# A four-layer graph attention network: other row tiles of layer 2 treated whole, and four early gathers for layer 3

## The chip, the core and the metric

The kernel runs on one core of one Trainium2 chip. The metric is the device time of the whole program in microseconds (us). The engines go by short names: PE is TensorE (PEld its weight loads), DVE is VectorE, ACT is ScalarE, POOL is GpSimd, and SP is the engine whose queue issues plain DMAs. POOL issues the indirect DMAs, called gathers here.

## The reference

A graph of 4096 nodes with 256 features goes through four attention layers, all over one adjacency matrix, in which about one entry in 256 is set, and the diagonal. Each layer adds the input to the attention's output and normalizes. Layers 0 and 1 have four heads of 64 features, layer 2 has two heads of 128. Layer 3 has one head in two signs. Cut to what matters:

```python
def attention(x, adj, ...):                 # layers 0, 1, 2, per head
    e = leaky_relu(s1[:, None] + s2[None, :], 0.2)     # s1, s2: x times learned vectors
    att = softmax(where(adj > 0, e, -huge), axis=1)
    return att @ (x @ W)

def layer3(x, adj, W, a, fc_W):
    e = leaky_relu(Wh1 + Wh2.T, 0.2)
    pos = softmax(where(adj > 0, e, -huge), axis=1)
    neg = -softmax(where(adj > 0, -e, -huge), axis=1)
    return elu(concatenate([pos @ x, neg @ x], axis=1) @ fc_W)

x = layernorm(x + layer_n(x, adj))          # n = 0, 1, 2, 3
```

## The kernel before

**Row tiles, lists, gathers.** The 4096 nodes are 32 row tiles of 128 nodes. As the adjacency is sparse, a row tile needs only the nodes that at least one of its rows is joined to. Beside layer 0 the kernel makes, for every row tile, a list of up to 13x128 such nodes (`lists`), and a packed mask, `maskC`. In a layer a row tile has 14 positions of 128 nodes: 13 are gathered from the table `vals` by the list (L634, POOL), and position 6 (`FRONT`) is the tile's own 128 rows (L631, SP). Positions 0 to 6 are the first half, 7 to 13 the second. The lists are ordered so that positions 0 to 5 name only nodes of row tiles 0 to 16 (`MIX` is 17, `NODES` bounds the source of the gather); the others may name any node. For a half, ACT and DVE make the weights `w` (in layer 3: L664, L665, L667 on ACT, L666, L668 on DVE), and PE multiplies them with the gathered rows (L699 in layers 2 and 3). In layer 3 a first half holds the matmuls of head 1 and then those of head 0, 14 records in the profile for each.

**Whole blocks.** In layers 2 and 3 some row tiles are not gathered but computed against all 4096 nodes, four row tiles (a block) at a time, with a full mask `maskW`. `WHOLE` says how many blocks at the end of the range are treated so: three in layer 2 (row tiles 20 to 31) and one in layer 3 (28 to 31). `whole_rows` yields units, one for each of 32 node tiles (L927 to L938), and `half_with_whole` spreads them over the layer's half steps. While `lists` runs, `places` writes the mask of each such block to DRAM (L392).

**Steps and projections.** A layer walks its gather tiles in half steps, numbered 2m and 2m+1 for the m-th gather tile. A finished row tile is normalized, alone or in groups (`GROUPS`: pairs of an end and a size, looked up by row tile), and joins `ready`. A `Projection` makes its row of the next layer's `vals` table: two transposes (L536, PE), a copy (L541, ACT), the matmuls (L550, PE), the row (L568 to L576, ACT and DVE), its write (L578, SP), then the transposed edge terms (L582, L588, L589). `half_with_whole` starts at most one projection in each half step, in order of `ready`.

**From layer to layer.** `close` ends a layer: it projects what is ready of row tiles below 17, loads the next layer's first half of tile 0, finishes the last tile, computes that half, projects the rest, then loads and computes the first half of tile 1 and loads those of tiles 2 and 3. Second halves are loaded in the steps that follow. Gathered rows land in slots: `g0` has 16, `g1` has 14. In layer 2 a slot holds two positions, in layer 3 one; first halves draw from `g0`, second halves from `g1`, in rotation.

The order written here gives the priorities. Where each engine's and each queue's instructions really stand was fixed when the program was built, by a scheduler that estimates when an instruction can go; on the chip every engine and queue then works strictly in that order.

Of the kernel before, what the change touches and what calls it, by code (L numbers as in the profile page):

```python
# [53 lines left out]
NT = N // P  # L54
KT = F // P
BT = 4
# [16 lines left out]
CAP = NG * P  # L73
HALF = NP // 2

GROUPS = (((24, 4),), ((28, 2),), ((16, 2), (20, 1), (31, 2)), ((28, 1), (31, 4)))
LEAD = 10
MIX = 17
FRONT = 6
# [15 lines left out]

WHOLE = (0, 0, 3, 1)

LEAST = 2.0611536224385579e-09  # L100

# [76 lines left out]
class Turns:  # L178


    def __init__(self, pools):
        self.pools = list(pools)
# [6 lines left out]
class Program:  # L189
# [98 lines left out]
    def lists(self, ctx):  # L288
# [75 lines left out]
        class Block:  # L364
# [23 lines left out]

            def places(self):
                blk = self.blk  # L390
                if blk >= NB - max(WHOLE):
                    nc.sync.dma_start(out=shared["maskW"][blk], in_=self.mk)  # L392
                hit = wk.tile([P, BT, NT], BF16, name="hit")
                nc.vector.tensor_scalar(hit, self.red, 0.0, None, op0=ALU.is_gt)
                flat = hit.rearrange("p t j -> p (t j)")
                nc.vector.memset(flat[:, blk * BT:blk * BT + (BT - 1) * (NT + 1) + 1:NT + 1], 0.0)
                pt = prog.bank(prog.pthree)
                nc.tensor.matmul(pt[:, :P], flat, ones, start=True, stop=True)
                totals = wk.tile([P, P], BF16, name="totals")
                nc.scalar.copy(totals, pt[:, :P])  # L400
                pq = prog.bank(prog.pthree)
                nc.tensor.matmul(pq[:, :P], tri, flat, start=True, stop=False, skip_group_check=True)
                nc.tensor.matmul(pq[:, :P], totals, bt.rearrange("p t j -> p (t j)"), start=False, stop=False,
                                 skip_group_check=True)
                nc.tensor.matmul(pq[:, P:P + BT], totals, tot, start=False, stop=True, skip_group_check=True)
                ms = slice(blk * BT, (blk + 1) * BT)
                self.place = wk.tile([P, BT, NT], F32, name="place")
                here = self.place
                nc.vector.tensor_tensor(here, pq[:, :P].rearrange("p (t j) -> p t j", t=BT), lo[:, ms, :],
                                        op=ALU.subtract)  # L410
                nc.vector.tensor_tensor(here, here, hit, op=ALU.mult)
                nc.vector.tensor_copy(total[:, ms], pq[:, P:P + BT])

                for col in (wid[:, ms, :], None):
                    off = wk.tile([P, BT, NT], F32, name="off")
                    if col is None:
                        nc.vector.tensor_scalar(off, here, 0.0, None, op0=ALU.is_lt)
                    else:
                        nc.vector.tensor_tensor(off, here, col, op=ALU.is_gt)
                    nc.vector.tensor_tensor(bad, bad, off, op=ALU.max)  # L420
# [177 lines left out]
class RowTile:  # L598

    def __init__(self, layer, m):
        self.layer, self.m = layer, m
        self.slots = {}
        self.accs = None

    def place(self, pos):


        L, n = self.layer, self.layer.n  # L610
        per = 1 if n == 3 else 2
        s = pos // per
        if s not in self.slots:
            pool = L.prog.g1 if n > 0 and s * per >= HALF else L.prog.g0
            self.slots[s] = pool.tile([P, 2 * ROW[0]], F32, name="G")
        c = (pos % per) * ROW[n]
        return self.slots[s][:, c:c + ROW[n]]
# [20 lines left out]
    def half(self, half):  # L638
# [1 line left out]
        prog, sh, S = L.prog, L.shared, self.S  # L640
        H, Wd, V, T, A = HEADS[n], WIDTH[n], VALS[n], TERMS[n], LOGS[n]
        if self.accs is None:
            pool = prog.ptwo[1 if n == 3 and self.m % 2 else 0]
            self.accs = [prog.bank(pool) for _ in range(2 if n == 3 else 1)]
        accs = self.accs
        G = [self.place(half * HALF + k) for k in range(HALF)]
# [75 lines left out]
class Layer:  # L722
# [2 lines left out]

    def __init__(self, prog, n):
        self.prog, self.n, self.nc, self.shared = prog, n, prog.nc, prog.shared
        self.count = NT - WHOLE[n] * BT
        self.tiles = {}
        self.loaded = set()  # L730
        self.units = self.whole_rows()
        self.total = WHOLE[n] * NT * (1 if n < 3 else 2)
        self.used = 0
        self.nxt = self.middle = self.stored = self.between = None
        self.group = []
        self.ready = []
        self.step = 0
        self.last = ()


    def tile(self, m):
        if m not in self.tiles:
            self.tiles[m] = RowTile(self, m)
        return self.tiles[m]

    def load(self, m, half):
# [63 lines left out]
    def half_with_whole(self, m, part):  # L810

        proj = None
        self.step = 2 * m + part
        if self.ready and self.ready[0][0] < self.step:
            _, y, row = self.ready.pop(0)
            self.set_banks()
            proj = Projection(self.prog, self.n + 1, self.nxt, y, row)
            proj.transpose()
        with ExitStack() as order:
            for ins in self.last:  # L820
# [27 lines left out]
    def close(self, following):  # L848
# [11 lines left out]
            self.set_banks()  # L860
            Projection(self.prog, self.n + 1, self.nxt, *entry[1:]).all()
        if following is not None:
            following.load(0, 0)
        if WHOLE[self.n]:
            for _ in self.units:
                pass
# [26 lines left out]
    def whole_rows(self):  # L893
        n, nc, prog, sh = self.n, self.nc, self.prog, self.shared
        H, Wd, T = HEADS[n], WIDTH[n], TERMS[n]
        groups = [range(H)] if n < 3 else [(0,), (1,)]
        for blk in range(NB - WHOLE[n], NB):
            tiles = range(blk * BT, (blk + 1) * BT)
            S = prog.bk.tile([P, T, BT, P], F32, name="Sw")
            for it, m in enumerate(tiles):  # L900
# [589 lines left out]
```

## Time and profile before

| what | value |
|---|---|
| median of three runs | 2287.78 us (2284.84 to 2289.15) |
| profiled execution | 2288.18 us |
| its span, first to last instruction | 2286.4 us |
| mean granted clock of PE | 0.961 |
| PE busy | 2026.1 us, 89% |
| PEld busy | 1835.8 us, 80% |
| DVE busy | 1798.3 us, 79% |
| ACT busy | 1741.5 us, 76% |
| POOL busy | 1493.2 us, 65% |
| gathers (L634) | 1456, mean 1017 ns |

The matmuls (L699) of layer 2's gathered half steps run from 1358.0 to 1751 us, and layer 3 fills the rest. A line of a timeline reads: start in us, duration in us (of all, where several instructions are merged), engine, line of the kernel, operation, output <- input, number of instructions, and in brackets the idle time of the engine just before with what ended it. SPq is SP's queue; its time is that of issuing a DMA, not of moving the data.

### The profile page before, as it was taken

The numbers are of one execution on the slowest core, as the hardware profiler recorded it, in microseconds if no ns is written. First come the engines' busy times: TensorE is split into PE (matmuls) and PEld (weight loads), VectorE is DVE, ScalarE is ACT, GpSimd is POOL, SyncE is SP. The second block draws the span as 40 slices with busy tenths as digits, with TensorE's granted clock in tenths as the row PEclk, the third lists the DMA queues.
The fourth block names the chain that finished last, engine by engine and source line by source line (L and its number), as shares of the span: only waits on it lengthen the run. The fifth ranks groups of instructions, "written<-read, shape, count | busy, mean of one in ns | idle before, by whom it ended". The sixth has DMA issues, their size and how long they took to land.

```text
span 2286.4 us, 49074 instructions
## 1 busy us (share of the span) xinstructions
PE 2026.1 (89%) x15689; PEld 1835.8 (80%) x15689; DVE 1798.3 (79%) x5317; ACT 1741.5 (76%) x4977; POOL 1493.2 (65%) x1596
## 2 busy tenths in 40 slices
PE   4888888988999968998889898989998799999996
PEld 2667877877889958998888887989997688888885
DVE  2898998989999968998888895887885365566566
ACT  4778887977789958988788886988883666676664
POOL 2117664646567777777777777777761677777773
PEclk7999999999999989999999999999999899999998
DMA  8889777866456765666666666778764788888884
GB/s 279 257 262 349 219 231 250 282 201 212 143 155 188 208 181 158 190 182 165 177 170 172 176 168 176 221 213 233 217 201 139 243 268 274 270 259 282 261 255 139
DMA packets 250320, 493.00 MB, mean 216 GB/s; under 512 B 44385, under 2 KB 156610, under 8 KB 249666
## 3 DMA queue, kind: packets, MB, share of 16 engines
q0 software_dynamic: 81536, 245.30, 38.0%
q1 hardware_dynamic: 168514, 244.46, 33.5%
q8 instruction: 126, 2.06, 0.4%
q14 instruction: 144, 1.18, 0.2%
HBM read 437.05 MB, written 52.54 MB: 214 GB/s over the span
## 4 chain that ended last, share of the span: by engine, by line
PE 51%; DVE 15%; DMA 14%; ACT 11%; issue 5%; POOL 3%; SPq 0%; DVEq 0%; ACTq 0%; POOLq 0%
PE bank L699 16%; PE bank L696 14%; PE bank L938 10%; DMA G<-vals,idx 8%; ACT w L687 6%; PE bank L550 5%; PE bank L442 4%; POOL G L634 3%; DVE w L688 3%; DMA raw<-in_adjB_dram 2%; DVE w L684 2%; DVE oh L436 2%; DVE w L678 1%; DMA G<-vals 1%; ACT mk L380 1%
## 5 line engine op out<-in xcount | busy, mean ns | idle before, releaser
L634 POOL DMA_INDIRECT G<-vals,idx x1456 | 1480.2, 1017 | 754.2 <-issue 205.0
L687 ACT ACTIVATE w<-S,G 128x128 f32<-128x128 f32 x3248 | 988.2, 389 | 122.9 <-DMA G<-vals,idx 106.8
L696 PE MATMUL bank<-w,G 128*65 128x128 f32 x7168 | 842.9, 277 | 102.0 <-DVE w L684 79.0
L696 PEld LDWEIGHTS bank<-w,G 128*65 128x65 f32 x7168 | 800.6, 140 | 120.8 <-DVE w L684 91.3
L699 PE MATMUL bank<-G,w 128*128 128x257 f32 (+1 forms) x2688 | 491.3, 340 | 33.6 <-DVE w L666 11.8
L699 PEld LDWEIGHTS bank<-G,w 128*128 128x128 f32 x2688 | 431.8, 193 | 83.5 <-DVE w L666 14.7
L688 DVE SCALAR_TENSOR_TENSOR w<-w,bank 128x896 f32<-128x896 f32 x384 | 411.7, 1081 | 21.0 <-ACT w L687 20.5
L938 PE MATMUL bank<-vw,pw 128*128 128x129 f32 (+1 forms) x2048 | 301.2, 304 | 6.6 <-issue 3.2
L938 PEld LDWEIGHTS bank<-vw,pw 128*128 128x128 f32 x2048 | 276.9, 193 | 23.7 <-issue 3.7
L664 ACT ACTIVATE w<-S,G 128x128 f32<-128x128 f32 x392 | 140.0, 391 | 128.7 <-DMA G<-vals 64.3
L436 DVE TENSOR_SCALAR oh<-iota,place 128x256 bf16<-128x256 f16 (+2 forms) x992 | 225.7, 304 | 14.7 <-PE bank L442 14.1
L442 PE MATMUL bank<-mk,oh 128*128 128x132 fp8e4 x2336 | 188.5, 224 | 18.1 <-DVE oh L436 9.2
L550 PE MATMUL bank<-wext,xT 128*128 128x268 f32 (+3 forms) x640 | 181.5, 415 | 16.4 <-ACT xT L541 14.4
L678 DVE TENSOR_TENSOR w<-S,G 128x256 f32<-128x256 f32 x384 | 154.4, 418 | 51.8 <-DMA G<-vals,idx 48.9
L442 PEld LDWEIGHTS <-oh 128*128 128x128 bf16 x2336 | 144.2, 98 | 58.8 <-DVE oh L436 27.3
L380 ACT ACTIVATE mk<-raw 128x1024 uint8<-128x1024 int32 x128 | 130.7, 1053 | 25.8 <-DMA raw<-in_adjB_dram 25.7
L550 PEld LDWEIGHTS bank<-wext,xT 128*128 128x128 f32 x640 | 118.4, 203 | 35.6 <-ACT xT L541 16.9
L927 ACT ACTIVATE pw<-Sw,d 128x512 f32<-128x512 f32 x192 | 131.6, 714 | 17.0 <-PE bank L938 12.7
L935 DVE TENSOR_TENSOR pw<-pw,mw 128x512 f32<-128x512 f32 x64 | 44.0, 692 | 124.3 <-ACT pw L934 65.6
L928 DVE SCALAR_TENSOR_TENSOR pw<-pw,mw 128x512 f32<-128x512 f32 x192 | 126.9, 692 | 18.2 <-ACT pw L927 17.4
L684 DVE SCALAR_TENSOR_TENSOR w<-w,bank 128x896 f32<-128x896 f32 x128 | 138.7, 1083 | 0.9
L688 DVE SCALAR_TENSOR_TENSOR w<-w,mk 128x896 f32<-128x896 f32 x80 | 86.7, 1087 | 43.1 <-ACT w L687 42.0
(131 smaller groups left out, 1605.0 us busy)
## 6 DMA issues: line engine op xcount, KB each, us to landing
raw<-in_adjB_dram SPq DMA_DIRECT2D x128, 512.0 KB
mk<-maskC SPq DMA_DIRECT2D x112, 231.0 KB
G<-vals,idx POOLq DMA_INDIRECT x1456
S<-edge SPq DMA_DIRECT2D x64, 256.0 KB
vw<-vals SPq DMA_DIRECT2D x96, 129.0 KB
xp<-y SPq DMA_DIRECT2D x96, 128.0 KB
y<-xp SPq DMA_DIRECT2D x96, 128.0 KB
mw<-maskW SPq DMA_DIRECT2D x20, 528.0 KB
```

Of the source, the lines that this page charges most:

```text
L380: nc.scalar.activation(mk[:, q:q + 2, :, :P], src, AF.Copy, scale=EDGE)
L436: nc.vector.tensor_scalar(oh[:, :n * P], iota[:, :n * P], self.place[:, it, j:j + 1], None, op0=ALU.is_equal)
L442: nc.tensor.matmul(accs[b][:, s * MC:(s + 1) * MC], oh[:, (k - a) * P:(k - a + 1) * P], mk[:, j, it, :].bitcast(FP8), start=touches[b][0] ...
L550: nc.tensor.matmul(pp[:, :c1 - c0], self.xT[:, k, :], wext[:, k, c0:c1], start=(k == 0), stop=(k == KT - 1 and brow is None))
L634: nc.gpsimd.indirect_dma_start(out=self.place(pos), out_offset=None, in_=sh["v"][n][:NODES[t], :], in_offset=bass.IndirectOffsetOnAxis(ap= ...
L678: nc.vector.tensor_tensor(w[h][:, k:k + 2, :], S[:, h:h + 1, :].to_broadcast([P, 2, P]), dd[:, :, V + T + h:V + T + h + 1].to_broadcast([P ...
L684: nc.vector.scalar_tensor_tensor(w[h], w[h], LEAST, mh, op0=ALU.max, op1=ALU.mult)
L687: nc.scalar.activation(w[h][:, k, :], S[:, h, :], AF.Exp, bias=d(k, h))
L688: nc.vector.scalar_tensor_tensor(w[h], w[h], LEAST, mh, op0=ALU.max, op1=ALU.mult)
L696: nc.tensor.matmul(accs[0][:Wd, h * P:(h + 1) * P], v, w[h][:, k, :], **how)
L699: nc.tensor.matmul(a, w[h][:, k, :], v, **how)
L938: nc.tensor.matmul(accs[it][:, c:c + Wd], p[:, it, :], v[:, c:c + Wd], start=(j == 0 and h == heads[0]), stop=(j == NT - 1), skip_group_ch ...
```

## The change

Three things change.

`WHOLE` now names blocks: 3, 6 and 7 in layer 2, that is row tiles 12 to 15 and 24 to 31. The gather tiles of layer 2 are row tiles 0 to 11 and then 16 to 23, still 20 of them. `ORDER` translates a step into a row tile. The masks written by `places` are those of blocks 3, 6 and 7. The groups of the norm are chosen anew.

`half_with_whole` takes, of the tiles that are ready, those below 17 first.

`close` of layer 2 loads four first halves at once, those of layer 3's tiles 0 to 3. For this, layer 3's slots are dealt anew: tiles 0 and 1 have both halves in `g0`, tiles 2 and 3 have the first half in `g1` and the second in `g0`, and from tile 4 on even tiles are all in `g1`, odd ones all in `g0`.

```diff
-GROUPS = (((24, 4),), ((28, 2),), ((16, 2), (20, 1), (31, 2)), ((28, 1), (31, 4)))
+GROUPS = (((24, 4),), ((28, 2),), ((16, 2), (17, 1), (22, 2), (24, 1), (31, 2)), ((28, 1), (31, 4)))
...
-WHOLE = (0, 0, 3, 1)
+WHOLE = ((), (), (3, 6, 7), (7,))
+ORDER = tuple([m for m in range(NT) if m // BT not in w] for w in WHOLE)
...
-                if blk >= NB - max(WHOLE):
+                if any(blk in w for w in WHOLE):
                     nc.sync.dma_start(out=shared["maskW"][blk], in_=self.mk)
...
         if s not in self.slots:
-            pool = L.prog.g1 if n > 0 and s * per >= HALF else L.prog.g0
+            if n == 3:
+                other = self.step % 2 == 0 if self.step > 3 else self.step > 1 and s < HALF
+            else:
+                other = n > 0 and s * per >= HALF
+            pool = L.prog.g1 if other else L.prog.g0
             self.slots[s] = pool.tile([P, 2 * ROW[0]], F32, name="G")
...
-        self.count = NT - WHOLE[n] * BT
+        self.order = ORDER[n]
+        self.count = len(self.order)
...
-            self.tiles[m] = RowTile(self, m)
+            self.tiles[m] = RowTile(self, m, self.order[m])
...
-        if self.ready and self.ready[0][0] < self.step:
-            _, y, row = self.ready.pop(0)
+        able = sorted((e for e in self.ready if e[0] < self.step), key=lambda e: e[2] >= MIX)
+        if able:
+            self.ready.remove(able[0])
             self.set_banks()
-            proj = Projection(self.prog, self.n + 1, self.nxt, y, row)
+            proj = Projection(self.prog, self.n + 1, self.nxt, *able[0][1:])
...
         if following is not None:
-            following.load(0, 0)
+            for m in range(4 if following.n == 3 else 1):
+                following.load(m, 0)
...
-        for blk in range(NB - WHOLE[n], NB):
+        for blk in WHOLE[n]:
```

More of the change, by code (lines that the diff above doesn't have):

```diff
@@ L598, with __init__ @@
 class RowTile:
-    def __init__(self, layer, m):
-        self.layer, self.m = layer, m
+    def __init__(self, layer, step, m):
+        self.layer, self.step, self.m = layer, step, m
         self.slots = {}
@@ L642, in half @@
         if self.accs is None:
-            pool = prog.ptwo[1 if n == 3 and self.m % 2 else 0]
+            pool = prog.ptwo[1 if n == 3 and self.step % 2 else 0]
             self.accs = [prog.bank(pool) for _ in range(2 if n == 3 else 1)]
@@ L731, in __init__ @@
         self.units = self.whole_rows()
-        self.total = WHOLE[n] * NT * (1 if n < 3 else 2)
+        self.total = len(WHOLE[n]) * NT * (1 if n < 3 else 2)
         self.used = 0
```

## The prediction

> **What bounds the kernel now.** The page came first. Its slice view (40 slices of 57.16 us) shows where an engine falls out of its pattern:
>
> ```profile
> PE   4888888988999968998889898989998799999996
> POOL 2117664646567777777777777777761677777773
> ```
>
> POOL, which issues all gathers, has one hole between its first gathers and its end: slice 31, 1715 to 1772 us. Layer 2 ends there and layer 3 begins. The windows view puts both sides of it in numbers (busy time of PE, PEld, DVE, ACT, POOL, then granted clock, DMA share, GB/s):
>
> ```profile
> 1700.00:1725.00 25.00, 25.00 (x217) 24.69 (x216) 17.50 (x49) 16.64 (x47) 3.75 (x3) 1.00 0.47 139
> 1725.00:1750.00 25.00, 24.92 (x192) 23.69 (x191) 21.76 (x129) 7.80 (x27) 0.00 (x0) 1.00 0.36 113
> 1750.00:1775.00 25.00, 15.96 (x61) 10.45 (x59) 8.88 (x38) 7.39 (x21) 9.91 (x11) 0.80 0.62 181
> 1775.00:1800.00 25.00, 21.57 (x88) 17.82 (x88) 10.77 (x21) 17.03 (x32) 14.55 (x14) 0.86 0.70 216
> 1800.00:1825.00 25.00, 16.86 (x69) 13.81 (x67) 6.97 (x10) 15.99 (x31) 19.21 (x20) 0.86 0.86 263
> 1825.00:1850.00 25.00, 24.95 (x115) 21.90 (x116) 18.86 (x61) 20.01 (x49) 19.40 (x19) 1.00 0.79 244
> ```
>
> Up to 1750 us PE is full. Then it is busy for only 15.96, 21.57 and 16.86 of 25 us, and DVE and ACT are no fuller: something is late. The timelines of POOL and of SP's queue say what:
>
> ```profile
> 1702.80 1.85 POOL L634 DMA_INDIRECT G<-vals,idx  x1 [0.30 <-issue]
> 1762.04 0.94 POOL L634 DMA_INDIRECT G<-vals,idx  x1 [57.39 <-DMA y<-xp]
> ...
> 1787.79 0.95 POOL L634 DMA_INDIRECT G<-vals,idx  x1 [0.30 <-issue]
> 1795.54 1.14 POOL L634 DMA_INDIRECT G<-vals,idx  x1 [6.79 <-issue]
> ```
>
> ```profile
> 1758.22 0.32 SPq L578 DMA_DIRECT2D vals<-row  x1
> ...
> 1791.99 0.37 SPq L578 DMA_DIRECT2D vals<-row  x1
> ```
>
> After layer 2's last gather POOL stands still for 57.4 us. Layer 3's first gather starts 3.82 us after the row write at 1758.22, which is that of row tile 16, the last of the tiles that a first half may read. POOL issues 20 gathers, stands again for 6.79 us, and goes on 3.55 us after the row write at 1791.99: that of row tile 19, the last of all, which every second half must wait for. (Which tile a row belongs to follows from counting projections through the half steps: tile 16 is the first projected in `close`, 31, 17, 18 and 19 come behind.) From 1795.54 on the list of waits holds for POOL
>
> ```profile
> POOL G L634 <- PE bank L699: 36.9, 121, 0.3
> POOL G L634 <- issue: 31.5, 82, 6.8
> ```
>
> and twelve lines like them (us in total, times, longest): but for the 6.8 us just named, no pause is longer than 0.3 us. Of layer 3's 28x13 = 364 gathers, 344 run from 1795.54 to 2257.27 us, (2257.27-1795.54)/344 = 1.342 us each, and 29 us of tail follow. PE is nearly as full, yet POOL never stands: the end of the kernel is the start of POOL's unbroken run, plus gathers left times 1.342, plus the tail. The Trainium skill (Perfetto Trace Analysis, "Identifying the Most-Contended Engine") ranks engines by occupancy, TensorE by its weight loads; in the last window above that is 21.90 of 25 us against POOL's 19.40, so the rule would name TensorE, which these waits contradict. By the rule the 2.3 us charged to POOL below would not count, and the gain would be that much larger.
>
> **Part 1: other whole blocks.** No instruction goes: 20 gather tiles and 96 units stay. Counting half steps by the code's rules, row tile 16 becomes gather step 12 instead of 16 and is projected in half step 29 instead of in `close`. Each half step projects at most one tile. Before, 27 of 32 projections fit into the steps and five remain (16, 31, 17, 18, 19); after, 28 fit and four remain (20, 21, 22, 23). The one more costs PE eight L550 matmuls (1.74 us), transposes and edge (0.36), 2.1 us, in steps where PE is full: step 39's last half ends at 1750.9+2.1 = 1753.0. The groups of the norm stay 18 in number; they cost nothing new.
>
> **Part 2: four first halves at once.** All rows that they read are written some ten half steps before `close`, so POOL waits only for slots, which layer 2's last four gather tiles give back between about 1726 and 1753 us. 24 gathers at 1.25 us (0.95 busy and 0.30 between) are 30 us, and fit into the hole before about 1765. The DMA share of 0.36 to 0.47 there leaves them room.
>
> What then starts POOL's unbroken run is again the last row write. The four projections left are a chain through two banks; their transposes follow each other in 4.21 us in the trace of before (1754.07, 1758.28, 1762.49), and a row's write is issued 4.13 us after its transposes (1758.28 to 1762.41). Before, tiles 17, 18 and 19 fell out of this rhythm (writes at 1770.26, 1778.42, 1791.99), since ACT stood in order at `w` L664 for gathers (24.1 us in 20 waits from 1745 to 1850) and PE ran at a clock of 0.75. These gathers are now there early. Three places for the last write:
>
> - the first-half matmuls fit into the chain's gaps: 1754.07+2.1+3x4.21+4.13 = 1772.9
> - tile 0's half, first in program order and now ready, stands ahead on PE with 6.07 us: 1779.0
> - tile 1's stands ahead as well: 1785.1
>
> I take the middle one, since program order puts only tile 0's half ahead of the four. With 3.55 us to the first gather, second halves start at 1776.5, **1782.6** or 1788.7. Before, 24 gathers were done, and the 25th began, at 1800.85. So POOL gains 24.4, **18.3** or 12.2 us.
>
> **Part 3: the slots.** From step 4 on a tile has 14 slots of one pool, and position p waits for the tile two before, position p (g1) or p-2 (g0), as now or easier. Only the start differs: tile 4's second half takes tile 3's first-half slots, where it took tile 2's second-half slots. Before, this was POOL's 59th gather at 1845.99. Tile 3's first half began on PE at 1844.82, and its second 14 of 28 matmul records, which read each slot last, free the first slot at 1844.82+3.03+0.43 = 1848.3. POOL stands 2.3 us, once; behind it stand all later gathers, and nobody else waits, as tile 4's second half comes on PE some 10 us after its data. On SP's queue the S, mask and own-row loads of tiles 1 to 3 move ahead with their gathers. They wait for buffers that ACT and DVE last read at 1729 and 1736 and for slots free by 1753, so the row writes behind them, of which the one that matters comes after 1765, are not held: I count nothing, and some 8 us (two projections) if SP stood until 1753 with rows behind it.
>
> **Part 4: one mask write moves.** Block 3's 2112 KB go out instead of block 5's. In the trace a `maskW` write is followed by a wait of ACT:
>
> ```profile
> 354.66 0.33 SPq L392 DMA_DIRECT2D maskW<-mk  x1
> ...
> 362.42 0.32 SPq L450 DMA_DIRECT2D maskC<-cm  x1
> ```
>
> ```profile
> 368.93 0.30 ACT L425 COPY cm<-mk 128x132 uint8<-128x132 uint8 x1 [5.71 <-DMA maskC<-cm]
> ```
>
> Such a wait, 5.7, 5.9 and 6.1 us, comes behind each of the three writes; one goes, worth 0 to 5.7 us. The new place is where block 3's totals are cast, 207 us:
>
> ```profile
> 205.00:210.00 5.00, 5.00 (x50) 4.96 (x49) 4.74 (x18) 4.38 (x7) 3.78 (x5) 1.00 1.06 384
> 210.00:215.00 5.00, 2.84 (x27) 2.58 (x26) 3.35 (x14) 0.78 (x2) 3.78 (x5) 1.00 1.04 388
> 215.00:220.00 5.00, 0.25 (x3) 0.01 (x1) 1.11 (x2) 4.24 (x13) 3.78 (x5) 0.83 1.02 386
> ```
>
> The DMA engines are full at 386 GB/s and PE nearly idle, waiting for adjacency. There 2.163 MB cost 2.163/0.386 = 5.6 us if nothing hides them, 0 if layer 0 makes it up later, and 5.6+6.0 if the same wait of ACT comes behind. I take 5.6 against 5.7: nothing, from -5.7 to +11.6. The skill's page DMA: Bandwidth & Descriptors ("Where 436 GB/s comes from") puts HBM's share of a core at about 358 GB/s and the fabric's ceiling at 435. The measured 386 passes the first; by it the write would be an estimated 6.0 us, and by the second an idle reserve of 49 GB/s would take part of it.
>
> **The sum**, against the profiled execution's own 2288.18 us (span 2286.4 and 1.78 around it; the median of the three runs, 2287.78, is 0.4 lower): -18.3 + 2.3 + 0 = -16.0, 2272.2 there and **2272 us** against the median.
>
> **The rivals.** *The last row is no earlier.* PE, ACT and DVE still give tile 23's row at 1792, because units and both first halves stand ahead of the projections. Then POOL starts at 1795.5 with 24 instead of 20 gathers done: -5.3+2.3 = -3, 2285 us, no change to be measured. For it: before, units of layer 3 (L930, L932 on ACT) already slipped between tiles 18 and 19. Against: much of that delay was ACT's wait for gathers.
>
> *Shared slots stop POOL.* This ends slower. First and second halves now draw on one pool; if the pause of 2.3 us comes not once but at every second tile, 12 times, it is 27.6-18.3 = +9.3, 2297 us. It decides from about ten pauses on ((18.3+4.6)/2.3). For it: POOL and PE run almost level, and the 59th gather has no margin. Against: position for position only the first round is tighter.
>
> *PE becomes the bound.* Before tile 0's second half (matmuls from 1815.52) seven units filled PE's holes. If fewer fit, seven times 1.73 us come later, and PE's slack in the run, 6.3 us where it waits for a gather at 1957, takes half: -16+6 = 2278.
>
> **How the numbers follow.** Forecast 0.62, PE as bound 0.15, last row no earlier 0.11, shared slots 0.12. The three runs span 4.3 us, so 0.2% (4.6 us) is about what can be told from no change. The forecast's own ends are -24.4+2.3-5.7 = -27.8 (2260) and -12.2+2.3+11.6 = +1.7 (2289); the far part of the upper end counts as no change. Faster 0.76, same 0.12, slower 0.12. The range goes from 2259 to 2286: it takes in the forecast's lower end, PE as bound and the unmeasurable rival, and leaves out the slower one and the forecast's worst mask write.
>
> **What would show it.** POOL's hole at slice 31 must hold 24 gathers ahead of the last row write. That write must lie near 1779, the next gather 3.5 us behind it, POOL then unbroken but for some 2 us near its 59th gather, its last gather near 2241. ACT's wait behind the first `maskW` write must be gone and the new one stand at about 207 us. A last row later than 1788, or pauses of POOL at every second tile, would prove me wrong.

## The result, and the profile after

The changed kernel takes 2286.56 us (median; 2281.53 to 2292.93) beside 2287.1 us for the kernel before on the same chip: ratio 0.9996, interval 0.9983 to 1.001. That is no change that can be measured; 2272 us was forecast. Its profiled execution took 2287.36 us with a span of 2285.6 us and a mean clock of 0.956. Eight of the runs that follow were on two other chips, on which the kernel before takes 2766 and 2763 us; their times are told only against the kernel before on the same chip.

The slices of the page (PE, then POOL) show that POOL's hole has become two half holes, slices 30 and 31, and PE is no fuller:

```profile
PE   4888898988999959999888996989998889999995
POOL 2117655556567777777777777777773477777773
```

The windows (busy PE, PEld, DVE, ACT, POOL; clock, DMA share, GB/s) show the early gathers: POOL has 15.71 and 12.48 us of work in the first two rows, where it had 3.75 and 0.00 before.

```profile
1700.00:1725.00 25.00, 25.00 (x211) 24.51 (x210) 15.65 (x31) 17.75 (x52) 15.71 (x13) 1.00 0.73 211
1725.00:1750.00 25.00, 21.31 (x152) 20.26 (x151) 20.41 (x111) 13.01 (x39) 12.48 (x12) 0.91 0.83 251
1750.00:1775.00 25.00, 21.23 (x120) 18.36 (x119) 12.72 (x56) 6.99 (x18) 3.89 (x4) 0.96 0.49 148
1775.00:1800.00 25.00, 24.19 (x108) 20.17 (x109) 12.69 (x30) 18.33 (x37) 1.89 (x2) 0.93 0.40 119
```

But PE now loses time already between 1725 and 1750 us (21.31 of 25, full before), and POOL has next to nothing to do from 1775 to 1797. The timelines of POOL and of SP's queue give the reason in three lines each:

```profile
1762.71 1.66 POOL L641 DMA_INDIRECT G<-vals,idx  x1 [6.44 <-ACT w L674]
1764.67 0.94 POOL L641 DMA_INDIRECT G<-vals,idx  x1 [0.30 <-issue]
1797.56 0.94 POOL L641 DMA_INDIRECT G<-vals,idx  x1 [31.95 <-DMA vw<-vals]
```

```profile
1765.86 0.32 SPq L580 DMA_DIRECT2D vals<-row  x1
1776.62 0.32 SPq L580 DMA_DIRECT2D vals<-row  x1
...
1794.28 0.32 SPq L580 DMA_DIRECT2D vals<-row  x1
```

All 24 first-half gathers are out by 1764.67, as forecast ("before about 1765"). Then POOL waits 31.95 us for layer 2's last row, whose write is issued at 1794.28: forecast 1779.0, and 1791.99 before. (The profile puts the wait down to `vw<-vals`, a load issued at 1795.05 that landed last; with both holds, below, it names `vals<-row` itself.) From 1797.56 on POOL runs without a pause over 0.6 us to its last gather at 2254.04; 340 gathers take (2254.98-1797.56)/340 = 1.345 us each, and 30.6 us of tail follow. So POOL's step 25 of layer 3 moved from 1800.85 to 1797.56, 3.3 us, and nothing more reached the end.

A line of ACT's list of waits between 1700 and 1815 us, ACT's timeline and PE's in the same place show what holds the row back:

```profile
ACT w L671 <- DMA G<-vals,idx: 20.4, 11, 4.9
```

```profile
1743.27 0.40 ACT L671 ACTIVATE w<-S,G 128x128 f32<-128x128 f32 x1 [3.13 <-DMA G<-vals,idx]
1745.15 0.40 ACT L671 ACTIVATE w<-S,G 128x128 f32<-128x128 f32 x1 [1.48 <-DMA G<-vals,idx]
...
1746.11 0.15 ACT L570 ACTIVATE row<-bank 128x2 f32<-128x2 f32 x1
...
1759.13 0.40 ACT L671 ACTIVATE w<-S,G 128x128 f32<-128x128 f32 x1 [4.31 <-DMA G<-vals,idx]
```

```profile
1746.99 0.37 PE L584 MATMUL bank<-ident,row 128*1 128x128 f32 x1 [3.69 <-DVE row L578]
...
1770.61 0.38 PE L538 MATMUL bank<-ident,y 128*128 128x128 f32 x2
...
1777.61 0.63 PE L538 MATMUL bank<-ident,y 128*128 128x128 f32 x2
1778.03 2.22 PE L949 MATMUL bank<-vw,pw 128*128 128x257 f32 x6
```

L671 is layer 3's first step for a gathered position, here of tile 1. Of the 20.4 us, 9.2 us in 4 waits lie ahead of the last row write; the rest end from 1801.13 on, behind POOL's restart. These instructions stand in ACT's order ahead of `row` L570, a step of a projection of layer 2. They wait for a gather, the projection waits behind them, PE waits 3.69 us for the projection (`row` L578), and PE holds the end of layer 2 in its own order behind that. Further on, between the transposes L538 of the last four projections, stand matmuls L949: whole units of layer 3. From this came theory R: the last row sets the start of POOL's unbroken run and so the end, and it is late by two parts, ACT's waits ahead of layer 2's last half and units between the last four projections.

### The profile page after: what moved, and what is told of

Its sections match the earlier page's. It is cut to its first block, busy times and chain, and to the rows that moved or that the text cites. A ratio compares the mean times of both kernels' runs of the same rounds, so it can differ in the third digit from the quotient of the medians.

```text
span 2285.6 us, 49078 instructions
## 1 busy us (share of the span) xinstructions
PE 2028.3 (89%) x15689; PEld 1840.9 (81%) x15689; DVE 1798.9 (79%) x5317; ACT 1744.7 (76%) x4977; POOL 1501.1 (66%) x1596
## 5 line engine op out<-in xcount | busy, mean ns | idle before, releaser
L703 PE MATMUL bank<-w,G 128*65 128x128 f32 x7168 | 843.5, 277 | 97.1 <-DVE w L691 79.3
L706 PE MATMUL bank<-G,w 128*128 128x257 f32 (+1 forms) x2688 | 497.7, 343 | 39.9 <-DVE w L695 15.9
L706 PEld LDWEIGHTS bank<-G,w 128*128 128x128 f32 x2688 | 438.3, 196 | 89.3 <-DVE w L695 16.5
L949 PE MATMUL bank<-vw,pw 128*128 128x129 f32 (+1 forms) x2048 | 301.6, 303 | 7.8 <-ACT zw L1013 2.7
L949 PEld LDWEIGHTS bank<-vw,pw 128*128 128x128 f32 x2048 | 275.7, 193 | 25.0 <-ACT zw L1013 3.1
L671 ACT ACTIVATE w<-S,G 128x128 f32<-128x128 f32 x392 | 140.6, 392 | 139.2 <-DMA G<-vals,idx 86.7
L552 PE MATMUL bank<-wext,xT 128*128 128x268 f32 (+3 forms) x640 | 178.2, 409 | 11.5 <-ACT xT L543 9.1
L552 PEld LDWEIGHTS bank<-wext,xT 128*128 128x128 f32 x640 | 117.1, 201 | 28.6 <-ACT xT L543 10.4
```

Of the source, the lines that this page charges most:

```text
L552: nc.tensor.matmul(pp[:, :c1 - c0], self.xT[:, k, :], wext[:, k, c0:c1], start=(k == 0), stop=(k == KT - 1 and brow is None))
L671: nc.scalar.activation(w[0][:, k, :], S[:, 0, :], AF.Relu, bias=d(k, 0))
L703: nc.tensor.matmul(accs[0][:Wd, h * P:(h + 1) * P], v, w[h][:, k, :], **how)
L706: nc.tensor.matmul(a, w[h][:, k, :], v, **how)
L949: nc.tensor.matmul(accs[it][:, c:c + Wd], p[:, it, :], v[:, c:c + Wd], start=(j == 0 and h == heads[0]), stop=(j == NT - 1), skip_group_ch ...
```

## Experiments

**Holding back tile 1, the units, and both.** Each kernel is the changed one with an order put on ACT: tile 1's first half, or the first twelve units of layer 3, or both, may start on ACT only behind the last projection. All computation is kept. The three edits, where `latest` is the last ACT instruction of the latest projection:

```diff
-        nc.scalar.activation(erow[:T, :], self.pe[:T, :P], AF.Identity, ...)
+        one = nc.scalar.activation(erow[:T, :], self.pe[:T, :P], AF.Identity, ...)
+        self.prog.latest = one.ins
...                                   # tile 1 held, in close
-            following.tile(1).half(0)
+            with ExitStack() as order:
+                if following.n == 3:
+                    order.enter_context(self.prog.tc.issue_after(self.prog.latest))
+                following.tile(1).half(0)
...                                   # units held, in whole_rows
+                            with ExitStack() as order:
+                                if heads[0] == 0 and j < 12:
+                                    order.enter_context(prog.tc.issue_after(prog.latest))
-                            nc.scalar.activation(p, S[:, 0], AF.Relu, bias=d)
+                                nc.scalar.activation(p, S[:, 0], AF.Relu, bias=d)
```

They ran first on one of the two other chips. Expected of tile 1 held:

> Starts from the changed kernel; ACT's work for the first half of layer 3's tile 1 may stand on ACT only behind the last projection of layer 2. Theory R (the last row write starts POOL's unbroken run, and that run sets the end): in the changed kernel ACT waits 9.2 us for tile 1's gathers between layer 2's last projections, and layer 2's last half ends at 1762.8 us; here it ends near 1754, the last row write moves from 1794.3 to about 1784.5, POOL goes on near 1788, the time falls by about 10 us to 2277. Theory E (PE is the bound, the row write does not matter): the time stays within 4 us of 2286.6.

of the units held:

> Starts from the changed kernel; the first 12 units of layer 3's whole block may stand on ACT only behind the last projection of layer 2. Theory R: the last four projections come 4.2 us apart instead of 5.5 to 7.0, the last row write moves from 1794.3 to about 1787.5, the time falls by about 6 us to 2280. Theory E: the eight units that filled PE before 1800 us (8 x 1.73 = 14 us) come later and the time rises, to 2290 to 2300.

and of both:

> Both holds of k1 and k2 together. Theory R: last row write near 1778, POOL goes on near 1781, 24 gathers done before that, time 16 us lower, 2270; up to 6 us more if PE then becomes the bound because the units come later (2276). Theory E: 2286 to 2300.

There they took 0.9973 (0.9952 to 0.9993), 0.9973 (0.9951 to 0.9996) and 0.9962 (0.9943 to 0.9981) of the kernel before. The expected absolute times were for the first chip and say nothing here; the changed kernel was not beside them, so these runs show a gain and not yet where it comes from. Tile 1 and the units were run once more on the second of these chips,

> Only ACT's work for tile 1's first half is held behind the last projection. Both holds together gave 2277.45, 9.0 us below the changed kernel. Theory R with its two parts (ACT's waits for tile 1's gathers ahead of layer 2's last half; units of layer 3 between the last four projections): layer 2's last half ends some 9 us earlier than in the changed kernel, the last four projections stay at 5.5 to 7 us each, the last row is written at 1783 to 1786, and the time is 5 to 7 us below the changed kernel. Rival A (only ACT's waits matter): the whole 9 us, the same as both holds. Rival U (only the units matter): within 2 us of the changed kernel.

> Only the first twelve units of layer 3 are held behind the last projection. Theory R: layer 2's last half ends as late as in the changed kernel, the last four projections close up to some 4.5 to 5 us each, the last row is written at 1786 to 1789, and the time is 3 to 5 us below the changed kernel. Rival A (only ACT's waits matter): within 2 us of it. Rival U (only the units matter): the whole 9 us.

with 0.9958 (0.9938 to 0.9979) and 0.9973 (0.9947 to 0.9998): both intervals lie below 1, and the two can't be told from each other there. On chips where the kernel before takes 2287 to 2291 us, and with the changed kernel beside them, the three were run again.

Both held:

> The changed kernel with two holds: ACT's work for tile 1's first half, and the first twelve units of layer 3, stand behind the last projection. Theory R: the last four projections run at about 4.2 us each, the last row is written 10 to 16 us earlier than in the changed kernel, POOL's unbroken run starts as much earlier, and the time falls by 8 to 15 us against the changed kernel of this chip. Rival E (PE is the bound, since the work held back is done later on PE): within 3 us of the changed kernel, though the last row is earlier. Rival A (the delay is ACT's waits ahead of layer 2's last half, and holds behind it don't matter): -2 to -6 us.

Measured: 2277.45 us beside 2286.45 of the changed kernel and 2289.53 of the kernel before, 0.9948 (0.9929 to 0.9967) of the latter: 9.0 us below the changed kernel. The last row write on SP's queue and POOL's restart:

```profile
1779.95 0.32 SPq L580 DMA_DIRECT2D vals<-row  x1
```

```profile
1783.32 0.94 POOL L642 DMA_INDIRECT G<-vals,idx  x1 [28.74 <-DMA vals<-row]
```

The last row is written at 1779.95 and POOL restarts at 1783.32; the prediction had 1779.0 and 1782.6 for the changed kernel. The last half of layer 2 ends at 1752.5 (forecast 1753.0), and the transposes of the last four projections follow each other in 4.18, 4.21 and 5.09 us (forecast 4.21). In the one profile of the changed kernel on this chip the last half ends at 1760.3, the last row is written at 1792.19 and POOL restarts at 1795.59. ACT has no wait for a gather ahead of the last row any more. Rival E (no gain, as PE is the bound) falls: the time follows the restart, though not in full.

Tile 1 held alone:

> Only ACT's work for tile 1's first half is held behind the last projection. Theory R with two parts (ACT's waits ahead of layer 2's last half, units between the last projections): 5 to 7 us below the changed kernel of the same chip, layer 2's last half some 9 us earlier, the last four projections as far apart as in the changed kernel. Rival A (only ACT's waits matter): 9 us below it. Rival U (only the units matter): within 2 us of it.

Measured: 2281.05 us beside 2286.84 of the changed kernel, 5.8 less. ACT's waits for gathers ahead of the last row are gone (the 9.0 us of the list below all end from 1792.75 on, behind POOL's restart), and layer 2's last half ends at 1751.3, where it ends at 1763.2 and 1763.8 in the changed kernel's profiles on this chip; but the last four transposes stand at 1759.04, 1769.88, 1775.04 and 1780.67, even farther apart, as a step of a unit stands 6.4 us for a load there:

```profile
ACT w L672 <- DMA G<-vals,idx: 9.0, 12, 1.8
ACT pw L945 <- DMA Sw<-edge: 6.4, 1, 6.4
```

```profile
1785.51 0.32 SPq L580 DMA_DIRECT2D vals<-row  x1
```

The changed kernel has 1794.57 and 1795.06 on this chip. Units held alone:

> Only the first twelve units of layer 3 are held behind the last projection. Tile 1 held alone was 5.8 us below the changed kernel, both holds 9.0. Theory R (two parts that add): layer 2's last half as late as in the changed kernel, the last four projections some 4.5 to 5 us apart, and 2 to 4.5 us below the changed kernel of the same chip. Rival O (the parts overlap: units that are held give place to ACT's waits, or the other way round): within 1.5 us of the changed kernel, or 5 us and more below it.

Measured: 2283.01 beside 2287.03 of the changed kernel, 4.0 less. Here the last half ends late (1761.0) and ACT's waits stay (11.6 us in 5 waits for gathers ahead of the last row), but the last transposes are 4.12, 4.99 and 6.26 us apart, 15.4 us in all instead of 19.0:

```profile
1790.45 0.32 SPq L580 DMA_DIRECT2D vals<-row  x1
```

The steps do not stay at 4.2 us. Without the units PE is busy for only 3.54 and 4.05 us in the two windows of 5 us from 1775 to 1785, the granted clock in them is 0.53 and 0.50, and the eight matmuls L552 of a projection take 3.81 us, where they take 2.01 at 1769.96:

```profile
1779.40 3.81 PE L552 MATMUL bank<-wext,xT 128*128 128x256 f32 x8 [0.52 <-ACT xT L543]
```

5.8 and 4.0 make 9.8, both together gave 9.0. By the spread of the runs, an estimate, each of these differences is uncertain by some 3 to 5 us, so the times alone exclude "only the units" (within 2 us with tile 1 held) but not "only ACT's waits". The row writes are clearer: they come 9.3 us earlier with tile 1 held, 4.4 with the units held and 12.2 with both, each against the changed kernel on the same chip. So both parts are real and nearly add, as theory R has it.

**One gather in thirteen less.** Is it POOL, with its gathers, that sets the end? This kernel is the changed one without the gathers of position 13 in layer 3; position 12's rows are used in their place, so that part of the output is not computed. PE, ACT and DVE do all of their instructions.

```diff
         per = 1 if n == 3 else 2
+        if n == 3 and pos == NP - 1:
+            pos = NP - 2
         s = pos // per
...
             t = pos - (pos > FRONT)
+            if n == 3 and pos == NP - 1:
+                continue
```

> The changed kernel with the gather of position 13 left out in layer 3's 28 tiles (position 12's rows are used twice, so 28 gathers fewer, the same matmuls). Theory R: POOL's run is 340-28 = 312 gathers long, 28 x 1.345 = 37.7 us shorter; PE, with some 30 us of waits in the run, gives back what it can: the time falls by 20 to 38 us, to 2249 to 2267. Theory E: less than 5 us lower, 2282 to 2287.

> Layer 3 without the gathers of position 13 (28 of 364); the position before it is used twice, so PE, ACT and DVE do all of their work on data of another position. Theory R (POOL's unbroken run sets the end): 25 of the 28 fall into the run, 1.34 us each, so the time falls by 30 to 38 us against the changed kernel, while PE loses most of its idle stretches. Rival E (PE is the bound): 0 to -6 us. Between them, PE takes over when its idle time behind 1800 us (some 27 us in the profile of the changed kernel) is used up: -20 to -27 us.

One run fell on each of the two other chips: 0.9856 (0.9825 to 0.9888) and 0.9858 (0.9833 to 0.9883) of the kernel before, 43 and 39 us less; the changed kernel was not beside them. From the last row write to the last gather it takes 468.8 and 469.8 us, where the kernels with one hold or both take 508 to 511 us there, about 1.5 us a gather; 28 of them are 42, and 37.5 at 1.34 us. PE does its whole work in that shorter time (434.29 of 466 us busy from 2219 to 2685 us), so on those chips PE was not the bound, though the page gives its weight loads 72% of the span in that run and POOL 53%. The prediction set the rule of the Trainium skill (Perfetto Trace Analysis, "Identifying the Most-Contended Engine") aside for POOL's gathers; on those chips this measurement decides for the gathers.

It can't be carried over to the first chip as it is. POOL's run is not unbroken on the slower chips: it has pauses of up to 2.9 and 3.2 us with a gather left out and 3.6 us with both holds. And in the changed kernel on the first chip PE is busy for 430.74 of the 457.5 us from POOL's restart to its last gather, so by these numbers the same step could give at most some 27 us there, an estimate. It was not run there.

**Everything held.** Tile 0's first half, which the prediction had ahead of the last four projections, is put behind them too:

```diff
-            if following is not None:
+            if following is not None and following.n < 3:
                 following.tile(0).half(0)
...
                     order.enter_context(self.prog.tc.issue_after(self.prog.latest))
+                    following.tile(0).half(0)
```

> Both holds, and tile 0's first half is also put behind the last projection. The prediction had its 28 matmuls, some 6 us, ahead of the last four projections. Theory R: the last row is written another 5 to 7 us earlier than with both holds (1779.95 there), at 1773 to 1775, and the time is 2270 to 2274, 3 to 7 us below it. Rival E (PE becomes the bound, as the two first halves then stand ahead of the first second half on PE): the last row is earlier, but the time is within 2 us of both holds, and PE waits for no gather behind the restart. Rival W (the four projections fill PE no better without that half, as their chain through ACT and DVE is what takes the time): the last row comes within 2 us of 1780, and the time with it.

> Both holds, and tile 0's first half put behind the last projection. Theory R: the last row is written 5 to 7 us earlier than with both holds (1779.95 in the profile of that run), and the time is 12 to 16 us below the changed kernel of the same chip. Rival E (PE becomes the bound): the last row is earlier, but the time is that of both holds, 9 us below the changed kernel. Rival W (the chain through ACT and DVE takes the time, not PE): the last row is within 2 us of that with both holds, and the time as well.

On one of the two slower chips 0.9958 (0.994 to 0.9975) of the kernel before; then 2278.99 us beside 2286.84 of the changed kernel, 7.9 less, 0.995 (0.9931 to 0.9969) of the kernel before. That is not more than both holds give, and the numbers expected by R were missed. The row is far earlier, at 1769.72, with the transposes 4.21 us apart three times. POOL's timeline shows where the ten microseconds went:

```profile
1772.96 0.94 POOL L642 DMA_INDIRECT G<-vals,idx  x1 [22.56 <-DMA vals<-row]
1774.21 1.41 POOL L642 DMA_INDIRECT G<-vals,idx  x1 [0.30 <-issue]
1780.93 1.26 POOL L642 DMA_INDIRECT G<-vals,idx  x1 [5.32 <-PE bank L707]
...
1810.64 0.94 POOL L642 DMA_INDIRECT G<-vals,idx  x1 [2.17 <-PE bank L707]
```

After two gathers POOL stands for a matmul of layer 3. Tiles 0 and 1 have both halves in `g0` with 16 slots; their first halves hold 14, and now that they are computed late, only two are free. The last gather starts at 2239.52, against 2242.88 with both holds: of the 10.4 us by which POOL restarts earlier, 3.4 reach it. A wait for slots took the place of the wait for the row. W falls, as the row is earlier; E had the time right, but what takes the gain is this wait in the first 8 us behind the restart, and whether PE would have taken it otherwise was not tried.

**The parts of the change by themselves.** The other whole blocks alone, with one early load and the old slots (the changed kernel with these lines as before):

```diff
-            for m in range(4 if following.n == 3 else 1):
+            for m in range(1):
...
-            if n == 3:
-                other = self.step % 2 == 0 if self.step > 3 else self.step > 1 and s < HALF
-            else:
-                other = n > 0 and s * per >= HALF
+            other = n > 0 and s * per >= HALF
```

> The other whole blocks alone: of layer 3 only tile 0's first half is loaded ahead of layer 2's last half, and the slots are dealt as before. All rows below 17 are written early, so POOL can run ahead into layer 3 only as far as g0 reaches. Theory R: the last row write comes 3 to 9 us earlier than in the changed kernel, since tile 1's first half no longer stands on ACT between the last projections; but POOL has only 12 to 14 gathers done in the hole instead of 24, of which it makes up some as tile 0's first half gives its slots back: net -3 to +6 us against the changed kernel. Rival S (the blocks themselves cost time at the start of layer 2, and this is what ate the gain): the same as the changed kernel, within 2 us, or slower, with the first half steps of layer 2 later than in the kernel before. Rival E (PE is the bound): within 2 us.

Measured: 2289.98 us, 3.5 above the changed kernel of the same chip (ratio to before 0.9995, 0.9984 to 1.0006, where the changed kernel has 0.9989, 0.9977 to 1.0001; the two can't be told apart). The last row did not come earlier (1793.10), which theory R expected: tile 1's work stands on ACT between the projections here too, with 9.9 us in 4 waits for gathers ahead of the last row. Layer 2's last half ends at 1759.2, nearly as late as in the changed kernel of this chip (1760.3). So it is not the lines that load four first halves at once that put tile 1's work there; it comes with the other whole blocks, by which the rows below 17 are written early. At the restart 344 gathers are left instead of 340, and POOL pauses once for a slot, 2.08 us: by these numbers 4x1.34+2.1 = 7.5 us later, of which the times show 3.5. The four early loads and the new slots alone, on the kernel before (the reverse of these lines, with `self.m` for `self.step`):

> The four early loads and the new slots alone, on the blocks of the kernel before. Row tile 16, whose rows the first halves need, is then still projected behind layer 2's last half, so POOL's hole of some 57 us stays; 24 instead of 20 gathers may come ahead of the last row. Theory R: -5 to +3 us against the kernel before, the last row write where it was, or later by what ACT waits for gathers. Rival S (shared slots stop POOL at every second tile): +7 to +10 us, with pauses of POOL of 2 us and more at every second tile. Rival E: within 2 us.

Measured: 2292.24 us beside 2289.53 of the kernel before, 1.0006 (0.9995 to 1.0017). POOL's hole before layer 3 stays (56.08 us), 24 gathers come ahead of the last row, written at 1790.47, and POOL's pauses behind that are one of 1.99 us and none else over 0.4. Layer 2's last half ends in time, at 1750.0. Rival S falls: shared slots don't stop POOL at every second tile.

**One mask write more.** The kernel before, with block 3's mask written as well and never read:

```diff
-                if blk >= NB - max(WHOLE):
+                if blk >= NB - max(WHOLE) or blk == 3:
```

> The kernel before with one mask write more: block 3's 2112 KB go out as well, at the place where the changed kernel writes them (about 207 us in the kernel before), and are read by nobody. The prediction bounded this place by 0 and by 5.6 us of transfer plus 6.0 us of a wait of ACT. Theory H (hidden): layers 0 and 1 make it up, within 1.5 us of the kernel before. Rival D (the DMA engines are full there): +4 to +7 us. Rival D+W (the wait of ACT comes behind as well): +10 to +13 us.

Measured: 2292.56 beside 2291.0, 1.0008 (0.9993 to 1.0023), between -1.6 and +5.3 us. The wait of ACT together with the transfer (+10 or more) is excluded; the transfer alone is not quite, though 1.5 us lies near "hidden". The write goes out at 196.92 us, and these are the windows around it, first of the kernel before, then of this one:

```profile
215.00:235.00 20.00, 13.16 (x128) 12.36 (x127) 14.40 (x48) 17.14 (x42) 12.99 (x13) 0.83 0.97 328
```

```profile
215.00:235.00 20.00, 14.76 (x145) 14.06 (x146) 13.09 (x42) 16.73 (x39) 13.71 (x14) 0.84 1.03 384
```

384 instead of 328 GB/s over 20 us are 1.1 MB, half of the write: there was room behind the full stretch. ACT's wait for `maskC` at 212 us grows from 2.35 to 5.34 us, but PE's busy time from 195 to 255 us is 48.63 us beside 48.42.

**The changed kernel again,** as the yardstick of each chip:

> The changed kernel itself, as the yardstick of this chip for the other three. On the first chip it stood level with the kernel before (ratio 0.9996). Theory R (the write of layer 2's last row starts POOL's unbroken run of gathers, and that run sets the end): the last row write stands within 3 us of that of the kernel before, POOL resumes some 3.3 us behind it, and the ratio is 0.998 to 1.001. Rival E (PE is the bound): ratio the same, but PE then has no idle stretch behind POOL's restart. Both expect no change; the run only fixes the level.

> The changed kernel itself, as the yardstick of this chip for the two kernels with holds. Theory R: no change against the kernel before (0.9975 to 1.001), as the last row write comes no earlier in it. Rival C (chips differ in what the holds are worth, because the changed kernel itself differs): a ratio below 0.9975 here, and the holds worth less.

> The changed kernel itself beside it, as the yardstick. Its ratios so far were 0.9996, 0.9989 and 0.9981; pooled, a gain of about 2.5 us. Theory R: 0.9975 to 1.0005. The rival of the prediction that no row comes earlier had 24 instead of 20 gathers done and -3 us, which is 0.9987.

0.9989 (0.9977 to 1.0001), 0.9981 (0.9964 to 0.9998) and 0.9986 (0.9972 to 1.0). With the first result the four mean 0.9988, some 2.7 us less than before: below what one comparison can tell, and what the rival "the last row is no earlier" gave (-3). POOL restarts in these profiles at 1795.59, 1798.93 and 1797.89.

## Why the prediction was wrong

**What sets the end** held in the main. On the first chip and those like it POOL's run starts 3.0 to 3.9 us behind the last row write in the changed kernel and all its variants shown here (5.0 with the four loads alone), and the end moves with it, by part of the distance; on the slower chips one gather in thirteen less takes off what those gathers cost. That POOL alone sets the end on the first chip is argued from its pauses of 0.3 us: the chain that ended last, as the profile of the changed kernel follows it, lies for 61% of the time from 1800 us on in matmuls (L706 and L949), and PE has little idle time left.

**Part 1, the last half of layer 2,** is the first step that failed: forecast 1753.0, and 1762.9 in the changed kernel, 9.9 later. The 2.1 us for one projection more were fair: with tile 1 held it ends at 1751.3, with both holds at 1752.5. What was missing is tile 1's work on ACT between layer 2's last projections, in which ACT stands 9.2 us for tile 1's gathers. The prediction put tile 1's first half only behind tile 0's on PE ("program order puts only tile 0's half ahead of the four"). But program order is a priority, and each engine's order was fixed when the program was built. With the rows that they read written early, tile 1's gathers and its ACT work were placed ahead of layer 2's last projections; the other whole blocks alone, without the early loads, show the same, and the early loads alone do not. Those gathers were not "now there early" at all: POOL waited 5.0 us for a slot that layer 2's own last tiles hold before it issued the gather at 1755.33, ACT stood for a gather until 1759.13, and layer 2's last projections waited on ACT behind that. POOL's next wait, 6.4 us, is put down to tile 1's own `w` L674 and so follows from the delay.

```profile
POOL G L641 <- PE bank L706: 12.4, 6, 5.0
POOL G L641 <- ACT w L674: 6.4, 1, 6.4
```

These are POOL's waits from 1700 to 1765 us. "POOL waits only for slots" was written down, and that ACT waits with it was not.

**Part 2, the last four projections,** is the second: forecast 4.21 us apart, measured 7.00, 6.50 and 5.53, 6.4 more in all, with whole units of layer 3 between them. The prediction counted how these units fill PE's holes later; it did not place them here, except in the rival. With the units held the gaps shrink by 3.7 us and not by 6.4; there the clock is at 0.50 under the last of them. Tile 0's half stood ahead of the four as forecast; from the end of the last half to the first transposes it took 7.8 us where 9.2 were counted. So 9.9-1.5+6.4+0.5 (a write 4.64 instead of 4.13 us behind its transposes) = 15.3, which is 1794.28-1779.0. With both holds the row comes at 1779.95, where the forecast had 1779.0, in part by luck: the last half ends 0.5 us and the first transposes come 2.0 us earlier than forecast, the gaps take 0.9 us more, and the write comes 6.18 instead of 4.13 us behind its transposes, with the clock at 0.50 from 1775 to 1790 us.

**The step from POOL to the time** was a little too generous. With both holds POOL restarts 14.2 us earlier than the changed kernel's four profiles have it on average (1797.5; 12.3 against the one on the same chip), its last gather starts 10.5 earlier (7.6 on the same chip), the time is 9.0 lower. Two microseconds of it are one pause for a slot at 2018.87 us, and a gather with its pause takes 1.354 instead of 1.341 to 1.347 us on average. Nor is PE far behind: in both kernels it is busy for 100.00 of 100 us from 2100 to 2200 us. Against the kernel before, both holds give 12 of the 16 us forecast.

**Part 3:** the pause of 2.3 us at the 59th gather did not come (0.59 us once in the changed kernel). The slots' price appears instead where the first halves are computed late, 5.32 us.

**Part 4:** counted at nothing. The write of block 3 went out at 197.37 us, ten earlier than forecast. The extra write costs 1.5 us (-1.6 to +5.3) at its place, and ACT's wait behind the kernel before's first mask write (5.71 us) is gone in the first profile of the changed kernel, while 2.1 to 3.0 us of it stay in its other three. In all, up to 760 us, ACT's waits for `maskC` are 15.2 to 22.3 us in the four, and 23.6 before. Layer 2's gathered matmuls start 3.0 to 6.1 us earlier than in the profile of before (1352.0 to 1355.0 against 1358.0), which the forecast did not have; by the last half steps it is given back. Where layer 2 loses it was not tried.

**The rivals.** "The last row is no earlier" came true, with its own number (-3, 2285) and its own mechanism (units and first halves ahead of the projections); it was given 0.11. What spoke against it, "much of that delay was ACT's wait for gathers", should have spoken for it: the cure assumed that moved gathers take their consumers' waits away, when they let the consumers be placed earlier. It was also read too large: of the "24.1 us in 20 waits" of the kernel before only 7.0 us in 7 waits lie ahead of its last row write at 1791.99; the other 17 us could not delay that row. And the 6.3 us of "PE's slack" at 1957 us, in the rival on PE, are the time of one gather in the profile's chain; PE's idle time there is 0.79 us, ahead of 1961.94. A fair chance would have left the range open to 2290.

## What to carry to other kernels

When data is loaded earlier, or can be, ask where its consumers will stand in each engine's fixed order, not only whether the data fits. An in-order engine that takes a waiting step of the next stage ahead of the last steps of this stage can lose on the critical chain what the earlier load gained; an explicit order behind the chain's last step brought back some 9 of the 14.6 us that were missing from the forecast, and the version with both holds (2277.45 us) beats both kernels. And when such a hold is added, look at what the held work keeps occupied, and at what it had kept busy: holding one half more made the row ten microseconds earlier and the kernel no faster, as POOL then stood for slots, and with the units held PE's clock was at 0.50 under the last projections.

## What the runs showed of the hardware

PE's granted clock was low in stretches in which PE stood still in between. With both holds PE is busy for 3.35, 3.08, 3.54 and 4.05 us in the four windows of 5 us from 1760 to 1780 us, and the clock is 1.00, 1.00, 0.56 and 0.50 in them; it stays at 0.50 until 1790, over a wait of 5.12 us for `w` that ends at 1785.18. The next 28 matmuls (L707) take 9.22 us, where the same 28 take 6.33 at 1798 us, with the clock back at 1.00. Over 25 us:

```profile
1775.00:1800.00 25.00, 18.49 (x61) 14.36 (x62) 7.77 (x12) 15.35 (x32) 13.03 (x13) 0.68 0.48 136
```

The two other chips take 21% longer over the kernel before, though one matmul of layers 0 and 1 takes only 289 ns there in the first profile of tile 1 held, instead of 277 in the changed kernel on the first chip, and a gather 1003 instead of 1022. In that profile these matmuls (L704) have 251.7 us of idle time before them, 182 of it put down to "issue", where on the first chip it is 97.1, most of it for `w`; the mean granted clock is 0.893 against 0.956. What lies behind that was not tried.
